# Where the gated layer takes the difference of candidate and old state: VectorE from PSUM, or GpSimd from SBUF

## The chip, the cores and the metric

The kernel runs on one core of one Trainium2 chip. The metric is the device time of one execution in microseconds (us), lower is better. Engines are named as in the profile: PE is TensorE (matmul), DVE is VectorE, ACT is ScalarE, POOL is GpSimd, SP is SyncE.

## The reference

Four layers work on `x` of 64 graphs x 256 nodes x 128 features, with one adjacency matrix `adj` of 256 x 256, all in fp32. Each layer normalizes over the features, applies a relu, runs a graph network and adds its result to `x`. Layer 0 is the gated one, with five steps; layers 1 and 2 multiply by `adj` and project; layer 3 scores every pair of nodes.

```python
# layer 0, five times; sigmoid and tanh gates
m  = einsum('nm,bmd->bnd', adj, h);  av = concatenate([m, m], -1)
u3 = h @ u3_w.T + u3_b
z  = sigmoid(av @ w3_w.T + w3_b + u3)
r  = sigmoid(av @ w4_w.T + w4_b + u3)
hv = tanh(av @ w5_w.T + w5_b + (r * h @ u5_w.T + u5_b))
h  = (1.0 - z) * h + z * hv            # = h + z * (hv - h)
...
# layer 3: s1, s2 are two projections of h, for each pair of nodes i, j
pre = s1[:, :, None, :] + s2[:, None, :, :] + b_lin
e   = einsum('bije,e->bij', leaky_relu(pre, 0.2), a) + adj
out = sigmoid(softmax(e, axis=2) @ h)
```

## The kernel before

Two graphs form a pair (`NB = 2`), so there are 32 pairs. For each pair a generator `front(p)` issues layers 0 to 2 and the projections of layer 3. It keeps the state of the gated layer as `hT`, features on partitions, 128 x 512 (two graphs of 256 nodes).

Then comes the bulk of the work, the pair scores of layer 3. For a pair of graphs there are 2 x 64 tiles `rl` of 128 x 2048 elements: the minimum or relu of a row of s1 against all of s2. A tile can be made by DVE in one instruction (L669), by ACT in eight (L682) or by POOL in eight (L689). PE multiplies a finished tile by the score vector in eight matmuls of 512 columns (L726). There are 13 tile buffers, of which DVE may hold 8, ACT 3 and POOL 2. When a block of rows is scored, a second generator `tail` does its softmax and writes the result.

One order of instructions for each engine is written out by a planner while the kernel is traced. It keeps a clock for each engine, books each operation with a cost (`ran(engine, us, ...)`; `ELEMENTS = 0.61` for an elementwise DVE operation on 512 columns, `TANH = 0.57`, 2.2 for a DVE tile, 1.8 for two of POOL's instructions), and always moves on the engine that is furthest behind. A `yield engine, t` in a generator means that its next operation goes to that engine and has its inputs at time t. Ready steps of a tail go first, then those of a front, the earlier pair first, and a tile only when no step is ready. So engines with little other work make more tiles. The fronts of later pairs are spread out between the tiles: a front has 109 steps, and step k is not given out before its due time, which spreads them over the scoring of 1.7 pairs, up to two steps ahead:

```python
    STEPS_OF_FRONT, SPREAD, AHEAD = 109, 1.7, 2
...
            due = STEPS_OF_FRONT * (scored[0] / (2 * SLOTS) - (key - 2)) / SPREAD
            if CHAINS[key][2] > due + AHEAD:
                return None
```

Fronts 0 and 1 start together before any tile exists. The others begin as the scoring goes on.

PSUM has eight banks of 128 x 512. Three of them (`spare`) rotate among all fronts and tails: `take()` gets one, `spare.append` gives it back with the time from which it is free. SBUF work tiles with `**SHORT` share 12 buffers.

In a step of the gated layer the bank `pr` holds first the reset gate's and then the update gate's sum, and `pv` the candidate's. ACT applies a tanh to each (L403 for the update gate, L406 for the candidate; the sigmoids are written as tanhs of half the argument). DVE takes the difference of candidate and old state (L411), multiplies it by the gate plus one (L415) and adds half of that to the old state, which gives the new `hT` (L419).

Of the kernel before, what the change touches and what calls it, by code (L numbers as in the profile page):

```python
# [9 lines left out]
AF = mybir.ActivationFunctionType  # L10
# [10 lines left out]
PE, DVE, ACT, POOL = ENGINES = (mybir.EngineType.PE, mybir.EngineType.DVE, mybir.EngineType.Activation, mybir.EngineType.Pool)  # L21
# [4 lines left out]
def kernel(  # L26
# [50 lines left out]
    nc = tc.nc  # L77
# [17 lines left out]
    clock = dict.fromkeys((PE, DVE, ACT, POOL), 0.0)  # L95
# [4 lines left out]
    def ran(engine, us, *after):  # L100
        start = max(clock[engine], 0.0, *after)
        if engine == ACT:
            behind[0] = max(0.0, behind[0] - (start - clock[ACT])) + 0.024 * us
        clock[engine] = start + us
        return clock[engine] + SEEN[engine] + (behind[0] if engine == ACT else 0.0)
# [6 lines left out]
    spare = [[b, 0.0] for b in banks[5:]]  # L112

    def take():

        spare.sort(key=lambda b: b[1])
        return spare.pop(0)

    def by_feature(b):
        return b.rearrange("p (b n) -> p b n", b=NB)  # L120

    def by_token(b):
        return b.rearrange("p (b c n) -> p b c n", b=NB, c=NC)
# [95 lines left out]
    bz, br, bh = gate_b[:, 0:1], gate_b[:, 1:2], gate_b[:, 2:3]  # L219
# [56 lines left out]
    def project(pp, w, t, start=True, stop=True):  # L276

        side_by_side(pp, w, flat(t), start, stop)

    def mix_nodes(pm, h, a):  # L280

        pm = by_feature(pm)
        for b in range(NB):
            for c in range(NC):
                side_by_side(pm[:, b, :], h[:, b, c, :], a[:, c, :], c == 0, c == NC - 1)
# [8 lines left out]
    def to_token(pt, ht):  # L294

        pt = by_token(pt)
        for b in range(NB):
            for c in range(NC):
                nc.tensor.transpose(pt[:, b, c, :], ht[:, b, c * P:(c + 1) * P], ident)  # L299
# [9 lines left out]
    def feat(name, **kw):  # L309
        return work.tile([P, NB, N], F32, name=name, **kw)  # L310

    def tok(name, **kw):
        return work.tile([P, NB, NC, D], F32, name=name, **kw)
# [8 lines left out]
    COPY, BIASED, TANH, ELEMENTS = 0.48, 0.58, 0.57, 0.61  # L322

    def norm(src, since, h):

        stats = work.tile([P, NB * NC, 6], F32, name="stats")
        mv = work.tile([P, NB * NC, 2], F32, name="mv")
        s, h = rows_of(src), rows_of(h)
        yield DVE, since
        for k in range(NB * NC):  # L330
            nc.vector.bn_stats(stats[:, k, :], s[:, k, :])  # L331
        for k in range(NB * NC):
            nc.vector.bn_aggr(mv[:, k, :], stats[:, k, :])  # L333
        nc.vector.tensor_scalar(mv[:, :, 0], mv[:, :, 0], -1.0, None, op0=OP.mult)  # L334
        t = ran(DVE, 1.12, since)
        yield POOL, t
        inverse_root(mv[:, :, 1], OP.add, LN_EPS)
        nc.gpsimd.tensor_mul(mv[:, :, 0], mv[:, :, 0], mv[:, :, 1])  # L338
        t = ran(POOL, 1.4, t)
        yield ACT, t  # L340
        for k in range(NB * NC):
            nc.scalar.activation(h[:, k, :], s[:, k, :], AF.Relu, bias=mv[:, k, 0:1], scale=mv[:, k, 1:2])  # L342
        return ran(ACT, 1.54, t)

    def copied(name, bank, t):

        c = feat(name, **(SHORT if name not in KEPT else KEPT[name]))
        nc.scalar.copy(c, by_feature(bank[0]))  # L348
        t = ran(ACT, COPY, t)
        spare.append([bank[0], t])  # L350
        return c, t
# [5 lines left out]
    def front(p):  # L357
# [8 lines left out]
        t = yield from norm(x0, 0.0, h)  # L366
# [4 lines left out]
        t = ran(PE, TURN, t, b[1])  # L371
        yield ACT, t
        hT, t_hT = copied("hT", b, t)
        for step in range(STEPS):
            yield PE, t_h, 1
            b = take()
            mix_nodes(b[0], h, adj_t)
            t = ran(PE, MIX, t_h, b[1])
            yield ACT, t
            mT, t_m = copied("mT", b, t)  # L380
            yield PE, t_m, 1
            pr = take()
            project(pr[0], u3t, hT, stop=False)
            project(pr[0], w4t, mT, start=False)
            t = ran(PE, 2 * PROJECT, t_m, t_hT, pr[1])
            yield ACT, t, 1
            r = take()
            nc.scalar.activation(r[0], pr[0], AF.Tanh, bias=br, scale=0.5)  # L388
            t = ran(ACT, TANH, t, r[1])
            yield DVE, t  # L390
            rh = feat("rh", **SHORT)
            nc.vector.scalar_tensor_tensor(rh, by_feature(r[0]), 1.0, hT, op0=OP.add, op1=OP.mult)  # L392
            t_rh = ran(DVE, ELEMENTS, t)
            spare.append([r[0], t_rh])
            yield PE, t_rh, 1
            project(pr[0], w34, mT, start=False)
            t_z = ran(PE, PROJECT, t)
            pv = take()
            project(pv[0], w5t, mT, stop=False)
            project(pv[0], u5t, rh, start=False)  # L400
            t = ran(PE, 2 * PROJECT, t_rh, pv[1])
            yield ACT, t_z
            nc.scalar.activation(pr[0], pr[0], AF.Tanh, bias=bz, scale=0.5)  # L403
            t_z = ran(ACT, TANH, t_z)
            yield ACT, t
            nc.scalar.activation(pv[0], pv[0], AF.Tanh, bias=bh, scale=1.0)  # L406
            t = ran(ACT, TANH, t)

            yield DVE, t
            d = feat("d", **SHORT)  # L410
            nc.vector.tensor_sub(d, by_feature(pv[0]), hT)  # L411
            t = ran(DVE, ELEMENTS, t)
            spare.append([pv[0], t])
            yield DVE, max(t_z, clock[DVE])
            nc.vector.scalar_tensor_tensor(by_feature(pr[0]), by_feature(pr[0]), 1.0, d, op0=OP.add, op1=OP.mult)  # L415
            ran(DVE, ELEMENTS, t_z)
            yield DVE, clock[DVE]
            hT_new = feat("hT", bufs=4)
            nc.vector.scalar_tensor_tensor(hT_new, by_feature(pr[0]), 0.5, hT, op0=OP.mult, op1=OP.add)  # L419
            hT = hT_new  # L420
            t_hT = ran(DVE, ELEMENTS)
            spare.append([pr[0], t_hT])
            yield PE, t_hT, 1
            b = take()
            to_token(b[0], hT)
            t = ran(PE, TURN, t_hT, b[1])
            if step < STEPS - 1:
                yield ACT, t
                h = tok("h", **SHORT)
                nc.scalar.copy(h, by_token(b[0]))  # L430
                t_h = ran(ACT, COPY, t)
                spare.append([b[0], t_h])
# [3 lines left out]
        t = ran(DVE, ELEMENTS, t)  # L436
# [8 lines left out]
        t = ran(PE, MIX, t_h, b[1])  # L445
# [5 lines left out]
        t = ran(PE, TURN, t_h, b[1])  # L451
        yield ACT, t
        hT, t = copied("hT", b, t)
# [3 lines left out]
        t = ran(PE, MIX, t_h, b[1])  # L457
        yield ACT, t
        c2T, t = copied("c2T", b, t)
# [3 lines left out]
        t = ran(PE, PRODUCTS, t, po[1])  # L463
# [7 lines left out]
        t = ran(DVE, ELEMENTS)  # L471
# [4 lines left out]
        t = yield from norm(x2, t, h)  # L476
# [3 lines left out]
        t = ran(PE, MIX, t, b[1])  # L480
        yield ACT, t
        yT, t = copied("yT", b, t)
# [3 lines left out]
        t = ran(PE, PRODUCT, t, po[1])  # L486
# [3 lines left out]
        t = ran(DVE, ELEMENTS, t)  # L490
# [3 lines left out]
        t = ran(ACT, COPY, t)  # L494
# [3 lines left out]
        t = ran(DVE, ELEMENTS, t)  # L498
        yield POOL, t
        inverse_root(rn, OP.max, NORM_EPS * NORM_EPS)  # L500
        t = ran(POOL, 1.25, t)
# [6 lines left out]
        t = ran(DVE, 1.04, t)  # L508
# [4 lines left out]
        t = yield from norm(x3, t, h3)  # L513
# [3 lines left out]
        t = ran(PE, TURN, t, b[1])  # L517
        yield ACT, t
        hT, t_hT = copied("hT3", b, t)
# [13 lines left out]
        t = ran(PE, 0.22, t_hT, b[1])  # L533
# [3 lines left out]
        t = ran(ACT, 0.2, t)  # L537
# [9 lines left out]
        t = ran(PE, PROJECT, t_hT, b[1])  # L547
# [5 lines left out]
        t = ran(PE, PROJECT, t_hT, b[1])  # L553
# [8 lines left out]
        t = ran(PE, PROJECT, t_hT, b[1])  # L562
# [180 lines left out]
    def begin_front():  # L743
        p = begun_fronts[0]
        load_x(p + 1)
        begin(p, front(p))
        begun_fronts[0] += 1
# [87 lines left out]
```

## Time and profile before

| | us |
|---|---|
| median of 3 runs (range) | 5335.91 (5334.29 to 5347.27) |
| profiled execution, its own time | 5333.93 |
| its span | 5332.2 |
| PE, DVE, ACT, POOL busy | 5222.4, 5206.3, 5123.7, 5140.8 |
| DVE tiles (L669), busy | 4469.3 in 2009 instructions |
| ACT tiles (L682), busy | 4410.4 + 149.3 in 11072 + 312 instructions |
| POOL tiles (L689), busy | 4765.8 in 5312 instructions |
| differences on DVE (L411), busy | 108.6 in 160 instructions |
| tanh of the candidate on ACT (L406), busy | 148.9 in 160 instructions |

A group's row names the line, the engine, the operation, the tiles written and read with their shapes and the count; then its busy time and the mean ns of one; then the idle time of the engine just before it and what ended it. Instructions of one engine overlap, so the mean length of one is more than what it takes of the engine's time.

### The profile page before, as it was taken

How to read it: one execution, taken by the hardware profiler on the slowest of the kernel's cores; microseconds unless marked ns; L12 is line 12 of the kernel's file. 1: busy time of each engine (PE TensorE's matmuls, PEld its weight loads, DVE VectorE, ACT ScalarE, POOL GpSimd, SP SyncE). 2: the span in 40 equal slices, each digit the busy share in tenths (PEclk: the TensorE clock that was granted, in tenths of full speed). 3: DMA queues.
4: the chain of work that ended last, by engine and by line, in shares of the span. 5: the costliest groups of instructions: out<-in, count | busy, mean ns of one | idle time of the engine just before them, and what ended most of it. 6: DMA issues, size and time to landing. Idle time of an engine off the chain costs nothing.

```text
span 5332.2 us, 139121 instructions
## 1 busy us (share of the span) xinstructions
PE 5222.4 (98%) x56085; PEld 1864.0 (35%) x56085; DVE 5206.3 (98%) x4316; ACT 5123.7 (96%) x13529; POOL 5140.8 (96%) x5958
## 2 busy tenths in 40 slices
PE   7999999999999999999999999999999999999998
PEld 2333333333333333333333333333333333333332
DVE  3999999999999999999999999999999999999998
ACT  3999999999999999999999999999999999999998
POOL 0999999999999999999999999999999999999999
PEclk8999999999999999999999999999999999999999
DMA  0000000000000000000000000000000000000000
GB/s 17 10 5 8 8 5 8 8 5 8 8 5 8 5 8 8 5 8 7 6 8 7 6 8 5 8 8 5 8 8 5 8 7 6 8 5 6 6 5 4
DMA packets 60344, 37.49 MB, mean 7 GB/s; under 512 B 4528, under 2 KB 59696, under 8 KB 59696
## 3 DMA queue, kind: packets, MB, share of 16 engines
q1 hardware_dynamic: 56592, 27.54, 2.3%
q8 instruction: 438, 7.18, 0.6%
q14 instruction: 210, 1.72, 0.1%
q10 hardware_dynamic: 3104, 1.05, 0.1%
HBM read 18.09 MB, written 10.49 MB: 5 GB/s over the span
## 4 chain that ended last, share of the span: by engine, by line
DVE 52%; PE 27%; POOL 12%; issue 6%; ACT 2%; DMA 0%; DVEq 0%; POOLq 0%; SPq 0%; ACTq 0%
DVE rl L669 43%; PE bank L726 17%; POOL rl L689 11%; PE bank L271 9%; ACT rl L682 2%; DVE bank L415 1%; DVE hT L419 1%; DVE d L411 1%; DVE stats L331 1%; DVE rh L392 1%; PE bank L299 1%; DVE mv L334 1%; DVE nmx L583 1%; DVE mv L333 0%; POOL mv L266 0%
## 5 line engine op out<-in xcount | busy, mean ns | idle before, releaser
L689 POOL TENSOR_SCALAR rl<-s2n,s1b 128x256 f32<-128x256 f32 x5312 | 4765.8, 928 | 9.2 <-ACT s1b L556 8.9
L669 DVE TENSOR_TENSOR rl<-s1a,bank 128x2048 f32<-128x2048 f32 x2009 | 4469.3, 2276 | 11.2 <-ACT s1a L565 11.2
L682 ACT ACTIVATE rl<-bank,s1b 128x256 f32<-128x256 f32 x11072 | 4410.4, 913 | 1.0
L726 PE MATMUL bank<-rl,win_n 128*32 128x512 f32 x21384 | 2647.7, 593 | 38.6 <-DVE rl L669 34.3
L726 PE MATMUL bank<-rl,win 128*32 128x512 f32 x11384 | 1503.3, 593 | 0.0
L726 PEld LDWEIGHTS bank<-rl,win_n 128*32 128x32 f32 x21384 | 680.9, 110 | 1509.6 <-issue 1203.9
L726 PEld LDWEIGHTS bank<-rl,win 128*32 128x32 f32 x11384 | 367.8, 110 | 749.2 <-issue 627.1
L271 PE MATMUL bank<-adj_t,h 128*32 128x256 f32 x5120 | 308.7, 381 | 3.9 <-ACT h L430 3.8
L271 PEld LDWEIGHTS bank<-adj_t,h 128*32 128x32 f32 x5120 | 166.2, 110 | 173.7 <-issue 54.8
L342 ACT ACTIVATE h<-x,mv 128x128 f32<-128x128 f32 x384 | 173.7, 653 | 35.4 <-POOL mv L338 35.0
L348 ACT COPY mT<-bank 128x512 f32<-128x512 f32 x160 | 147.6, 922 | 37.1 <-PE bank L271 28.0
L271 PE MATMUL bank<-hT,u3t 128*32 128x512 f32 x1280 | 167.6, 593 | 0.0
L271 PE MATMUL bank<-mT,w4t 128*32 128x512 f32 x1280 | 167.6, 592 | 0.0
L271 PE MATMUL bank<-mT,w 128*32 128x512 f32 x1280 | 166.8, 593 | 0.5 <-ACT bank L388 0.5
L271 PE MATMUL bank<-mT,w5t 128*32 128x512 f32 x1280 | 166.8, 593 | 0.3 <-DVE rh L392 0.2
L388 ACT ACTIVATE bank<-bank,gate_b 128x512 f32<-128x512 f32 x160 | 152.4, 953 | 14.8 <-PE bank L271 14.4
L271 PE MATMUL bank<-rh,u5t 128*32 128x512 f32 x1280 | 166.6, 592 | 0.0
L403 ACT ACTIVATE bank<-bank,gate_b 128x512 f32<-128x512 f32 x160 | 147.8, 924 | 13.3 <-PE bank L271 13.2
L406 ACT ACTIVATE bank<-bank,gate_b 128x512 f32<-128x512 f32 x160 | 148.9, 930 | 11.2 <-PE bank L271 11.0
L430 ACT COPY h<-bank 128x512 f32<-128x512 f32 x128 | 132.2, 1032 | 23.3 <-PE bank L299 23.2
L682 ACT ACTIVATE rl<-s2c,s1a 128x256 f32<-128x256 f32 x312 | 149.3, 902 | 0.0
L411 DVE TENSOR_TENSOR d<-bank,hT 128x512 f32<-128x512 f32 x160 | 108.6, 678 | 37.6 <-ACT bank L406 37.6
(116 smaller groups left out, 3319.9 us busy)
## 6 DMA issues: line engine op xcount, KB each, us to landing
xin<-in_x_dram SPq DMA_DIRECT2D x64, 128.0 KB, 2.3
lin<-row SPq DMA_DIRECT2D x32, 256.0 KB, 7.6
out_dram<-o SPq DMA_DIRECT2D x64, 128.0 KB, 1.8
row<-quarter SPq DMA_DIRECT2D x32, 64.0 KB, 1.5
w_raw<-in_L_gnn_w_w_dram ACTq DMA_DIRECT2D x3, 128.0 KB, 4.1
th_raw<-in_L_gnn_Theta_dram ACTq DMA_DIRECT2D x1, 320.0 KB, 3.4
adj_n<-in_adj_dram SPq DMA_DIRECT2D x1, 256.0 KB, 4.5
w_raw<-in_L_gnn_u_w_dram ACTq DMA_DIRECT2D x2, 64.0 KB, 3.3
```

Of the source, the lines that this page charges most:

```text
L271: nc.tensor.matmul(o[g:g + 32], w[:, g:g + 32], t, start=start, stop=stop, skip_group_check=True)
L342: nc.scalar.activation(h[:, k, :], s[:, k, :], AF.Relu, bias=mv[:, k, 0:1], scale=mv[:, k, 1:2])
L348: nc.scalar.copy(c, by_feature(bank[0]))
L388: nc.scalar.activation(r[0], pr[0], AF.Tanh, bias=br, scale=0.5)
L403: nc.scalar.activation(pr[0], pr[0], AF.Tanh, bias=bz, scale=0.5)
L406: nc.scalar.activation(pv[0], pv[0], AF.Tanh, bias=bh, scale=1.0)
L411: nc.vector.tensor_sub(d, by_feature(pv[0]), hT)
L430: nc.scalar.copy(h, by_token(b[0]))
L669: nc.vector.tensor_tensor(t, rows.to_broadcast(whole), ops["s2a"].unsqueeze(1).to_broadcast(whole), op=OP.min)
L682: nc.scalar.activation(t[:, g, b, :], (s2p if k else ops["s2c"])[:, b, :], AF.Relu, bias=ops["s1"][k][:, b, i:i + 1], scale=-1.0)
L689: nc.gpsimd.tensor_scalar(t[:, part, b, :], ops["s2n"][:, b, :], ops["s1"][1][:, b, i:i + 1], None, op0=OP.min)
L726: nc.tensor.matmul(pe[g * 32:(g + 1) * 32, :], w[:, k, 31 - r:63 - r], flat(t[:, g]), start=first, stop=(left[block] == 0), skip_group_che ...
```

## The change

For all pairs but the first, ACT writes the candidate's tanh to the SBUF tile `d` instead of back into the PSUM bank `pv`, and gives the bank back at that point. GpSimd, which the kernel has read and write SBUF alone, subtracts the old state from `d` in place. DVE's product follows, planned at the later of that and the update gate's tanh. The planner books the subtraction with 1.3 us on POOL. Pair 0 stays as it was.

```diff
             nc.scalar.activation(pr[0], pr[0], AF.Tanh, bias=bz, scale=0.5)
             t_z = ran(ACT, TANH, t_z)
             yield ACT, t
-            nc.scalar.activation(pv[0], pv[0], AF.Tanh, bias=bh, scale=1.0)
-            t = ran(ACT, TANH, t)
-
-            yield DVE, t
+
             d = feat("d", **SHORT)
-            nc.vector.tensor_sub(d, by_feature(pv[0]), hT)
-            t = ran(DVE, ELEMENTS, t)
-            spare.append([pv[0], t])
-            yield DVE, max(t_z, clock[DVE])
+            if p < 1:
+                nc.scalar.activation(pv[0], pv[0], AF.Tanh, bias=bh, scale=1.0)
+                t = ran(ACT, TANH, t)
+                yield DVE, t
+                nc.vector.tensor_sub(d, by_feature(pv[0]), hT)
+                t = ran(DVE, ELEMENTS, t)
+                spare.append([pv[0], t])
+            else:
+                nc.scalar.activation(d, by_feature(pv[0]), AF.Tanh, bias=bh, scale=1.0)
+                t = ran(ACT, TANH, t)
+                spare.append([pv[0], t])
+                yield POOL, t
+                nc.gpsimd.tensor_sub(d, d, hT)
+                t = ran(POOL, 1.3, t)
+            yield DVE, max(t, t_z)
             nc.vector.scalar_tensor_tensor(by_feature(pr[0]), by_feature(pr[0]), 1.0, d, op0=OP.add, op1=OP.mult)
-            ran(DVE, ELEMENTS, t_z)
+            ran(DVE, ELEMENTS, t, t_z)
             yield DVE, clock[DVE]
             hT_new = feat("hT", bufs=4)
             nc.vector.scalar_tensor_tensor(hT_new, by_feature(pr[0]), 0.5, hT, op0=OP.mult, op1=OP.add)
```

The number of steps of a front stays 109.

## The prediction

> **What bounds the kernel now.** I read the page first: its span, the busy row and the costliest groups.
>
> ```profile
> span 5332.2 us, 139121 instructions
> PE 5222.4 (98%) x56085; PEld 1864.0 (35%) x56085; DVE 5206.3 (98%) x4316; ACT 5123.7 (96%) x13529; POOL 5140.8 (96%) x5958
> L689 POOL TENSOR_SCALAR rl<-s2n,s1b 128x256 f32<-128x256 f32 x5312 | 4765.8, 928 | 9.2 <-ACT s1b L556 8.9
> L669 DVE TENSOR_TENSOR rl<-s1a,bank 128x2048 f32<-128x2048 f32 x2009 | 4469.3, 2276 | 11.2 <-ACT s1a L565 11.2
> L682 ACT ACTIVATE rl<-bank,s1b 128x256 f32<-128x256 f32 x11072 | 4410.4, 913 | 1.0
> L411 DVE TENSOR_TENSOR d<-bank,hT 128x512 f32<-128x512 f32 x160 | 108.6, 678 | 37.6 <-ACT bank L406 37.6
> ```
>
> All four engines look full. Three of them make the same thing, pair tiles for the attention scores, and the planner gives the next tile to whichever is free. A tile is one instruction on DVE and eight on ACT or POOL: 2009 + 1423 + 664 = 4096 tiles. Work taken off one engine is therefore refilled with tiles, and the question is the exchange rate. Next, the sums by stretch:
>
> ```profile
> core 0: us, PE busy (x) PEld busy (x) DVE busy (x) ACT busy (x) POOL busy (x), PEclk, DMA share, GB/s
> 1066.00:2132.00 1066.00, 1059.36 (x11424) 376.01 (x11426) 1062.65 (x870) 1047.34 (x2772) 1052.04 (x1218) 1.00 0.03 7
> 2132.00:3198.00 1066.00, 1057.77 (x11498) 378.60 (x11494) 1061.81 (x878) 1039.71 (x2751) 1055.11 (x1223) 1.00 0.03 7
> ```
>
> Between the start (no tiles before 113 us) and the last 270 us, DVE is 99.6% busy, POOL 98.8%, ACT about 98%, at full clock. Matmul busy time is no peak, so I counted PE's work at the pace of its unbroken runs in the timeline: 0.857 us per tile's eight 512-column matmuls, 1.73 per 32 of 256 columns, 0.90 per 32 of 128, 0.58 per four transposes. With the counts of the groups: 4305 + 443 + 180 + 186 = 5114 us. Taking out the first 133 us and the ragged last 270, PE has about 100 us (2%) to spare in the long stretch. DVE and POOL set the pace, PE is close behind.
>
> Durations overlap, so prices must come from start to next start. The timeline of DVE (start, length, ...):
>
> ```profile
> 2518.71 6.67 DVE L669 TENSOR_TENSOR rl<-s1a,bank 128x2048 f32<-128x2048 f32 x3
> 2525.30 0.16 DVE L609 RECIPROCAL rs<-sums 128x2 f32<-128x2 f32 x1
> 2525.38 0.67 DVE L411 TENSOR_TENSOR d<-bank,hT 128x512 f32<-128x512 f32 x1
> 2525.96 2.28 DVE L669 TENSOR_TENSOR rl<-s1a,bank 128x2048 f32<-128x2048 f32 x1
> ...
> 5001.14 0.68 DVE L411 TENSOR_TENSOR d<-bank,hT 128x512 f32<-128x512 f32 x1
> 5001.86 0.70 DVE L415 SCALAR_TENSOR_TENSOR bank<-bank,d 128x512 f32<-128x512 f32 x1
> ```
>
> A DVE tile is (2525.30 − 2518.71)/3 = 2.197 us. The difference takes 0.60 before other work (0.58 here; 0.60 is usual), and 0.72 when the product that reads it comes straight after. POOL and ACT in the same way:
>
> ```profile
> 2516.78 1.30 POOL L579 TENSOR_TENSOR sc<-sc,lin 128x512 f32<-128x512 f32 x1
> 2518.03 12.57 POOL L689 TENSOR_SCALAR rl<-s2n,s1b 128x256 f32<-128x256 f32 x14
> ...
> 2522.02 1.13 ACT L406 ACTIVATE bank<-bank,gate_b 128x512 f32<-128x512 f32 x1
> 2522.59 1.08 ACT L597 ACTIVATE wT<-bank 128x512 f32<-128x512 f32 x1
> ...
> 2531.16 1.37 ACT L556 ACTIVATE s1b<-bank,blin 128x512 f32<-128x512 f32 x1
> 2531.73 3.71 ACT L682 ACTIVATE rl<-bank,s1b 128x256 f32<-128x256 f32 x8
> 2534.58 1.44 ACT L565 ACTIVATE s1a<-bank,blin 128x512 f32<-128x512 f32 x1
> ```
>
> A POOL tile is 8 × 12.57/14 = 7.18 us, its two-input 128x512 add 1.25, an ACT tile 2534.58 − 2531.73 = 2.85.
>
> **The change part by part.** It touches pairs 1 to 31 at five steps each, 155 times. In the trace ten differences run before the first tile: five of pair 0 (unchanged) and five of pair 1, where DVE and POOL both stand idle much of the time. That leaves 150 in the tile stretch.
>
> *Removed from DVE.* In the DVE timeline 67 of the 150 are followed directly by their product (mean 0.71), 83 by other work (0.60): 47.8 + 49.7 = 97.5 us, or 97.5/2.197 = 44.4 tiles.
>
> *Added to POOL.* Its subtraction of two SBUF inputs isn't in the trace, but the add of the same shape and operands is (L579, 1.26 to 1.35 long, while DVE was saturated). I take its 1.25 us; the bounds are 1.15 and 1.40. 150 × 1.25 = 188 us = 26.1 tiles. Here a rule speaks against the change: the Trainium skill, "GPSIMD Engine Reference", section "Engine selection", wants elementwise work on VectorE, since two-input operations are about 2 times slower on GpSimd. The rows agree on the ratio (1300/678 = 1.92). By the rule alone the move adds 188 − 97.5 = 90 us of engine time, +30 us over three engines. But that treats all engine time as equal: on tiles POOL is 7.18/2.197 = 3.3 times slower than DVE, so POOL is better at the subtraction than at what it otherwise does. I go by the rows: +44.4 − 26.1 = +18.3 tiles.
>
> *ACT's tanh into SBUF.* The nearest rows by destination are the biased activations s1a and s1b: mean 1195 and 1109 ns against 930 for L406. The Trainium skill, "ScalarE: Activation LUTs", section "Step-by-step: what each stage is for", says that ScalarE reaches PSUM faster than SBUF. Priced by these means, 0.18 to 0.27 × 150 = 27 to 40 us of ACT, 9 to 14 tiles, most of the gain. But start to next start it is 0.57 for L406 and 0.57 for s1b: the difference is latency, covered by the next activation. I take 0, with +0.1 (15 us, 5 tiles) as the bad end and −0.05 as the good one; the latency is met again below.
>
> *Rate.* Making tiles at 1/2.197 + 1/7.18 + 1/2.85 = 0.945 per us, 18.3 tiles are 19.4 us.
>
> *New waits.* DVE's product now waits for POOL, with tiles and the next rows of gates queued behind it; POOL's subtraction waits for ACT, with its quarter tiles behind it; PE waits for both. Nearest row: DVE's maximum waiting for POOL's add in the long stretch, second line below. That is 3.2 us for some 62, 0.05 each, where the planner books 1.05 us against 1.25 measured; the subtraction is booked at 1.3. I take 0.03 × 150 = 4.5 us of DVE, 2 tiles, 2 us; the bounds are 0 and 0.18 (ACT waiting for POOL's norm, first line, 22.2 us for some 125).
>
> ```profile
> ACT h L342 <- POOL mv L338: 22.2, 28, 2.7
> ...
> DVE nmx L583 <- POOL sc L579: 3.2, 10, 0.8
> ```
>
> *Latency and banks.* The chain of a step gets about 2 to 3 us longer (1.3 on POOL, a partial POOL tile ahead of it, and the product must queue for DVE). I cost this at nothing: 109 steps of a front are spread over 1.7 pairs of scoring, about 2.5 us a step, and the tiles between product and new state in the timeline show chains being held back, not rushed. Were that cover gone, 5 × 2.5 us per pair would delay READY, and DVE would stop before L669; it does so once, at the start. The candidate's bank comes free after the tanh instead of after the difference, the update gate's is held about as much longer: even. No DMA moves, so SP's queue is untouched. Startup: pair 0 unchanged, 0.
>
> Sum: −19.4 + 2 = −17.4 us against the profiled execution's own 5333.9 (span 5332.2), so 5316.5. The median of runs is 2 us above it: 5319.
>
> **The rivals.**
> *More than the sum.* The plan books 0.61 for a difference that took 0.71 in 67 cases, so DVE runs behind its plan and PE waits for it: PE's loads waited 99.3 us for DVE tiles in the long stretch (209 times, of which about 0.3 each is mere pace) and 61.9 for the new state. If the change saves 15 us of these as well, 5304. Against: POOL takes on the same role.
> *PE and ACT take it up.* PE has 2% to spare, yet in the chain of waits it runs unbroken for tens of us. ACT idles about 100 us in the long stretch, much of it before copies out of banks that PE has not filled. If faster DVE production only adds to that, or the tanh costs ACT 0.1 more, half or less of the gain is left: 5326 to 5336.
> *POOL comes late (slower).* One mechanism: POOL almost never waits, so each delay on it lasts, and DVE now meets it 150 times. The exchange breaks even when DVE idles 18.3 × 2.197/150 = 0.27 us per product. If half a POOL instruction is lost each time (0.9/2 = 0.45), DVE loses 67 us, 31 tiles, and the kernel is +13 us: 5349. For it: 12 of 64 maxima already waited for POOL. Against: 0.05 us each.
> The edit does what it says for 31 of 32 pairs, so that it has no effect at all I give no share.
>
> **How the numbers follow.** Differences under 0.3% (16 us) can hardly be told from none here: the three runs lie within 13 us. The sum of the parts: 0.55, its own range 5309 to 5327; the line of 0.3% is at 5319.9, so 0.33 of it is faster and 0.22 the same. More than the sum: 0.17, faster. PE and ACT: 0.17, same. POOL late: 0.11, slower. Together 0.50, 0.39, 0.11. The range 5302 to 5338 leaves out POOL late and the far end of the gain.
>
> **What would show it.** Right: L411's subtraction as 155 POOL rows near 1300 ns and 5 on DVE; DVE tiles up by about 35 to 45 to some 2050, POOL's fall from 664 to about 640, ACT's nearly unchanged; DVE still over 99% busy; DVE's product waiting for POOL under 10 us; the tanh's next activation still 0.57 later. Wrong: the product waiting over 40 us for POOL; ACT's tiles falling by 15 or more; the POOL row over 1.5 us, or POOL tiles slower than 0.90 per instruction, which would mean that DVE slows it; more PE waits before banks.

## The result and the profile after

The changed kernel takes 5323.38 us (median of 14 runs, 5321.42 to 5333.19) against 5335.67 us for the kernel before (14 runs), a ratio of 0.9978 with a 95% interval of 0.9971 to 0.9985. That is 12.3 us or 0.23%: clear of noise, but on the near side of the 0.3% line.

Executions come in two paces of ACT and POOL, 0.1 to 0.3% apart as the last section shows, and the kernel's time differs by 7 to 13 us between them, so executions of the same pace are set against each other below. The profile of the changed kernel shown here (from the run after2) is of the faster pace, like that of before: span 5322.4 us, own time 5324.2 us.

The page's busy row, its costliest groups, and then ACT's smaller group of tiles, before (L682) and after (L690):

```profile
PE 5211.6 (98%) x56085; PEld 1855.6 (35%) x56085; DVE 5189.9 (98%) x4198; ACT 5092.5 (96%) x13465; POOL 5126.3 (96%) x5881
...
L697 POOL TENSOR_SCALAR rl<-s2n,s1b 128x256 f32<-128x256 f32 x5080 | 4559.9, 923 | 16.0 <-ACT s1b L564 9.5
L677 DVE TENSOR_TENSOR rl<-s1a,bank 128x2048 f32<-128x2048 f32 x2046 | 4545.1, 2275 | 11.9 <-ACT s1a L573 11.9
L690 ACT ACTIVATE rl<-bank,s1b 128x256 f32<-128x256 f32 x11304 | 4511.0, 893 | 2.0 <-PE bank L734 0.8
...
L682 ACT ACTIVATE rl<-s2c,s1a 128x256 f32<-128x256 f32 x312 | 149.3, 902 | 0.0
L690 ACT ACTIVATE rl<-s2c,s1a 128x256 f32<-128x256 f32 x16 | 7.6, 838 | 0.0
```

Counts are the first thing to read. DVE makes 2046 tiles instead of 2009, POOL 5080/8 = 635 instead of 664, and ACT the rest: 4096 − 2046 − 635 = 1415 instead of 1423. So DVE gains 37, POOL loses 29, and ACT loses 8.

The tiles are not quite one pool. They come in two halves of 2048, one for each half of the score's features (0 and 1), and the planner chooses the half for an engine:

```python
        return 0 if e == DVE or e == ACT and following[0] <= following[1] - LAG else 1
```

DVE makes tiles of half 0 only and POOL of half 1 only. ACT helps with half 0 when that is at least two tiles behind (`LAG = 2`). For those tiles it reads SBUF (`s2c`), for its others a PSUM bank. ACT made 312/8 = 39 tiles of half 0 before and makes 16/8 = 2 now, so DVE does its half nearly alone. By the medians from start to start in unbroken runs of tiles, an instruction of the SBUF form takes 399 ns and one of the PSUM form 356, so the 37 tiles fewer spare ACT 37 × 8 × 43 ns = 12.7 us.

Next the subtraction and what stands around it, from the groups of instructions by shape:

```profile
L420 POOL TENSOR_TENSOR d<-d,hT 128x512 f32<-128x512 f32 x155 | 199.9, 1290 | 67.5 <-ACT d L416 67.5
L416 ACT ACTIVATE d<-bank,gate_b 128x512 f32<-128x512 f32 x155 | 162.3, 1047 | 9.1 <-PE bank L271 9.0
...
L423 DVE SCALAR_TENSOR_TENSOR bank<-bank,d 128x512 f32<-128x512 f32 x160 | 110.4, 690 | 17.7 <-POOL d L420 17.3
```

155 subtractions of 1290 ns sit on POOL, as priced by the row of the score add. POOL's 67.5 us of idle time before them lie at the start, where it has nothing else to do. In the long stretch the waits are tiny (who waited, for whom: us, times, longest):

```profile
DVE bank L423 <- POOL d L420: 1.3, 5, 0.4
...
POOL d L420 <- ACT d L416: 1.1, 2, 0.6
```

The steps in the timeline, ACT's tanh and POOL's subtraction of one chain:

```profile
2549.22 1.03 ACT L416 ACTIVATE d<-bank,gate_b 128x512 f32<-128x512 f32 x1
2549.78 9.21 ACT L690 ACTIVATE rl<-bank,s1b 128x256 f32<-128x256 f32 x24
...
2552.18 1.28 POOL L420 TENSOR_TENSOR d<-d,hT 128x512 f32<-128x512 f32 x1
2553.44 7.19 POOL L697 TENSOR_SCALAR rl<-s2n,s1b 128x256 f32<-128x256 f32 x8
```

The tanh is longer than before, yet ACT's next activation starts 0.56 us after it (the median of 150 is 0.57, as before). POOL gives 1.26 us to the subtraction. Finally the long stretch by engine. First the kernel before, then the changed one:

```profile
133.00:5065.00 4932.00, 4892.88 (x52939) 1746.09 (x52935) 4911.33 (x4042) 4827.85 (x12763) 4876.95 (x5647) 1.00 0.03 7
```

```profile
133.00:5065.00 4932.00, 4896.07 (x53080) 1750.52 (x53084) 4912.61 (x3945) 4802.73 (x12714) 4869.02 (x5580) 1.00 0.03 7
```

The five busy times are PE, PE's weight loads, DVE, ACT and POOL. DVE's idle time is the same (4932 − 4911.3 = 20.7 us and 19.4). ACT's grew from 104.2 to 129.3 us (129.2 in a profile of the slower pace). This is where the experiments began.

### The profile page after: what moved, and what is told of

Its sections match the earlier page's. It is cut to its first block, busy times and chain, and to the rows that moved or that the text cites. A ratio compares the mean times of both kernels' runs of the same rounds, so it can differ in the third digit from the quotient of the medians.

```text
span 5331.4 us, 138379 instructions
## 1 busy us (share of the span) xinstructions
PE 5217.8 (98%) x56085; PEld 1858.3 (35%) x56085; DVE 5195.0 (97%) x4198; ACT 5101.5 (96%) x13465; POOL 5137.7 (96%) x5881
## 3 DMA queue, kind: packets, MB, share of 16 engines
q8 instruction: 438, 7.18, 0.6%
## 4 chain that ended last, share of the span: by engine, by line
DVE 41%; PE 37%; POOL 12%; issue 5%; ACT 4%; DMA 0%; POOLq 0%; DVEq 0%; SPq 0%; ACTq 0%
DVE rl L677 34%; PE bank L734 24%; PE bank L271 12%; POOL rl L697 11%; ACT rl L690 3%; DVE stats L331 1%; PE bank L299 1%; DVE hT L427 1%; DVE bank L423 1%; DVE rh L392 1%; DVE mv L334 1%; PE bank L292 0%; POOL d L420 0%; DVE nmx L591 0%; DVE sc L583 0%
## 5 line engine op out<-in xcount | busy, mean ns | idle before, releaser
L697 POOL TENSOR_SCALAR rl<-s2n,s1b 128x256 f32<-128x256 f32 x5080 | 4574.9, 942 | 14.9 <-ACT s1b L564 9.3
L677 DVE TENSOR_TENSOR rl<-s1a,bank 128x2048 f32<-128x2048 f32 x2046 | 4544.9, 2275 | 11.6 <-ACT s1a L573 11.6
L690 ACT ACTIVATE rl<-bank,s1b 128x256 f32<-128x256 f32 x11304 | 4520.1, 903 | 2.1 <-PE bank L734 0.9
L420 POOL TENSOR_TENSOR d<-d,hT 128x512 f32<-128x512 f32 x155 | 203.4, 1313 | 68.5 <-ACT d L416 68.5
L403 ACT ACTIVATE bank<-bank,gate_b 128x512 f32<-128x512 f32 x160 | 160.4, 1002 | 28.7 <-PE bank L271 28.5
L348 ACT COPY mT<-bank 128x512 f32<-128x512 f32 x160 | 141.1, 882 | 43.2 <-PE bank L271 21.6
L416 ACT ACTIVATE d<-bank,gate_b 128x512 f32<-128x512 f32 x155 | 164.5, 1061 | 9.3 <-PE bank L271 9.2
L388 ACT ACTIVATE bank<-bank,gate_b 128x512 f32<-128x512 f32 x160 | 151.4, 946 | 14.9 <-PE bank L271 10.6
L438 ACT COPY h<-bank 128x512 f32<-128x512 f32 x128 | 124.5, 973 | 21.6 <-PE bank L299 18.2
L266 POOL TENSOR_TENSOR mv<-mv,minus_half 128x4 f32<-128x4 f32 x128 | 133.2, 1041 | 10.7
```

Source lines behind the costliest of these rows:

```text
L266: nc.gpsimd.tensor_tensor(t, t, minus_half, op=OP.pow)
L416: nc.scalar.activation(d, by_feature(pv[0]), AF.Tanh, bias=bh, scale=1.0)
L420: nc.gpsimd.tensor_sub(d, d, hT)
L677: nc.vector.tensor_tensor(t, rows.to_broadcast(whole), ops["s2a"].unsqueeze(1).to_broadcast(whole), op=OP.min)
L690: nc.scalar.activation(t[:, g, b, :], (s2p if k else ops["s2c"])[:, b, :], AF.Relu, bias=ops["s1"][k][:, b, i:i + 1], scale=-1.0)
L697: nc.gpsimd.tensor_scalar(t[:, part, b, :], ops["s2n"][:, b, :], ops["s1"][1][:, b, i:i + 1], None, op0=OP.min)
```

## The experiments

Theory 1 (exchange): DVE, ACT and POOL set the pace, and whatever time one of them is spared becomes tiles at the rates of the prediction. Theory 2: PE is so near to full, or booked as so near to full, that the planner holds ACT back when DVE makes more tiles, and part of the gain ends as idle time of ACT. A tile waits in its buffer for PE, and ACT may hold three.

**The same kernel again.** No edit, for a profile at the pace of before.

> The changed kernel once more, for a second profile (the first profiled execution, 5333.2 us, lay 10 us above the median of the runs). Theory 1 (exchange: DVE, ACT and POOL all set the pace and freed time becomes tiles): about 5323 us again, ACT idle in the stretch 133 to 5065 us close to the 104 us of before. Theory 2 (PE, as the planner books it, is already full, so the planner holds ACT back): the same time, but ACT idle 20 to 40 us more than before.

Measured: 5324.2 us at the faster pace against 5335.9 for before on the same chip (11.6 us less), 5333.4 against 5348.9 at the slower one (15.5 us less). ACT idle in the stretch is 129.3 us in this execution, 25 us more than before, as theory 2 has it; the slower profile had shown as much, so this repeats a reading and tests nothing new.

**The subtraction left out.** DVE is relieved, POOL pays nothing.

```diff
-                yield POOL, t
-                nc.gpsimd.tensor_sub(d, d, hT)
-                t = ran(POOL, 1.3, t)
...
-    STEPS_OF_FRONT, SPREAD, AHEAD = 109, 1.7, 2
+    STEPS_OF_FRONT, SPREAD, AHEAD = 104, 1.7, 2
```

> The changed kernel with the subtraction left out for pairs 1 to 31: the product reads the tanh itself (front of 104 steps, so that the spread stays). DVE is relieved as in the change and POOL pays nothing. Theory 1: 44 tiles / 0.945 per us = 47 us under before, 5289 us. Theory 2: freed time ends as idle time of ACT; 10 to 25 us under before (5311 to 5326), ACT idle up by 80 us or more.

Measured: 5316.4 us at the faster pace (one execution, 19.5 us under before), 5323.7 at the slower (25.2 under). Theory 1 fails: less than half of the 47 us came. Its profile says where the rest went:

```profile
133.00:5065.00 4932.00, 4901.69 (x53198) 1755.98 (x53202) 4912.49 (x3949) 4751.89 (x12551) 4858.37 (x5627) 1.00 0.03 7
```

ACT idles 4932 − 4751.9 = 180.1 us, 76 more than before (theory 2 had 80 or more). At 2.85 us a tile that is 26.7 tiles, or 26.7/0.945 = 28 us of the kernel. The gap between 47 and 19.5 is 27.5.

**The other half alone.** POOL pays, DVE is not relieved.

```diff
+            if p >= 1:
+                yield POOL, t
+                e = feat("e", **SHORT)
+                nc.gpsimd.tensor_sub(e, d, hT)
+                ran(POOL, 1.3, t)
             yield DVE, max(t_z, clock[DVE])
...
-    STEPS_OF_FRONT, SPREAD, AHEAD = 109, 1.7, 2
+    STEPS_OF_FRONT, SPREAD, AHEAD = 114, 1.7, 2
```

> The kernel before, and beside its difference on DVE a second one on POOL for pairs 1 to 31 into a tile that nothing reads (front of 114 steps). POOL pays as in the change and DVE is not relieved. Theory 1: 26.1 tiles / 0.945 = 28 us over before, 5363 us. Theory 2: ACT was being held back and takes the tiles over; 10 to 22 us over before, ACT idle below 104 us.

Measured: 5371.0 us, 22.1 over before at the same (slower) pace, at the upper end of what theory 2 had and under the 28 of theory 1. ACT makes 1438 tiles instead of 1423, but its idle time falls only from 104 to 97 us. At this pace −25.2 and +22.1 add to −3, while the change itself brings −15.5. With fixed exchange rates the two halves would add up to the change; they don't.

**PE booked at the trace's pace.** Only the planner's numbers change, on the changed kernel, on the kernel before, and on the changed kernel a second time.

```diff
-    PROJECT, MIX, TURN, PRODUCT, PRODUCTS = 0.86, 1.74, 0.69, 0.88, 2.64
+    PROJECT, MIX, TURN, PRODUCT, PRODUCTS = 0.855, 1.715, 0.59, 0.875, 2.62
```

> The changed kernel with PE's operations booked in the planner at the pace that the trace shows (0.855, 1.715, 0.59, 0.875, 2.62 instead of 0.86, 1.74, 0.69, 0.88, 2.64); the work is the same. Theory 1: no change, within 5 us of 5323. Theory 2: the planner sees room on PE and lets ACT make more tiles: 10 to 25 us faster than the change (5298 to 5313), ACT idle falls by 30 us or more.

Measured: 5323.7 us at the slower pace, 9.7 us under the changed kernel there. ACT idle is 97.5 us instead of 129.3. The order alone is worth 10 us, as theory 2 says.

> The kernel before with PE's operations booked in the planner at 0.855, 1.715, 0.59, 0.875, 2.62. Compared with the changed kernel so booked, and with the kernel before at the same pace of ACT and POOL. Theory 2 (the tight booking of PE is what eats part of the change's gain): before gains less from the new booking than the changed kernel's 10 us, 0 to 5 us, and the change is then worth 17 to 22 us. Rival: the booking helps both alike, before gains 8 to 12 us, and the change stays worth 10 to 15 us.

> The changed kernel with that booking once more, to stand beside pe_before on the same chip. Theory 2: 17 to 22 us under pe_before. Rival: 10 to 15 us under it.

Measured, both at the slower pace: the kernel before goes from 5346.6 to 5339.3 us (7.3 less; ACT idle 86.7 us in its profile, which is of the faster pace), the changed one to 5323.6. So the change is worth 15.7 us with the new booking and 15.5 with the old one. Here my expectation failed: the loose booking costs both kernels about alike and is not what ate the change's gain. If theory 2 holds, it must be through PE's real load.

**PE made lighter.** One product of the gated layer is left out in all pairs (137 us of PE work in all): in the kernel before, in the changed kernel, and in the one without the subtraction.

```diff
-            project(pr[0], w34, mT, start=False)
-            t_z = ran(PE, PROJECT, t)
+            t_z = t_rh
```

> The kernel before with one PE product of the gated layer left out in all pairs (the update gate's w34 times mT, eight 512-column matmuls a step, 160 x 0.858 = 137 us of PE). It is the base for light_after and light_nodiff. Theory 2 in its wider form (PE is so close to full that the queue of finished tiles in front of it holds ACT back): 10 to 20 us faster than before, ACT idle in the stretch down from 104 us to 90 or less. Theory 1: no more than 3 us faster, since PE isn't what sets the pace.

> The changed kernel with the same PE product left out. Theory 2: with room on PE the change keeps what the exchange rates give, 15 to 20 us under light_before, and ACT's idle time no longer grows with it. Theory 1: the same 12 to 15 us as without the lighter PE.

> no_diff (the subtraction left out for pairs 1 to 31, tanh into SBUF) with the same PE product left out. This tells the theories apart best: with PE as it was, leaving the subtraction out was worth 20 to 25 us instead of the 47 us of the exchange. Theory 2: 40 to 50 us under light_before, ACT idle not above light_before's by more than 15 us. If something other than PE holds ACT back: again 20 to 28 us, with ACT idle up by 60 us or more.

All ran at the faster pace, with before at 5335.7 us:

| with the lighter PE | us | to light_before | the same edit with full PE, faster pace | ratio to before (95%) |
|---|---|---|---|---|
| light_before | 5324.5 | | | 0.9980 (0.9972 to 0.9987) |
| light_after | 5302.9 | −21.6 | −12.3 | 0.9938 (0.9925 to 0.9950) |
| light_nodiff | 5276.5 | −48.1 | −19.5 | 0.9889 (0.9876 to 0.9903) |

The long stretch of light_before, then of light_after, then of light_nodiff:

```profile
133.00:5065.00 4932.00, 4809.39 (x51820) 1727.27 (x51816) 4916.24 (x4050) 4846.79 (x12827) 4875.94 (x5647) 1.00 0.03 7
```

```profile
133.00:5065.00 4932.00, 4830.18 (x52060) 1742.98 (x52056) 4913.70 (x3942) 4854.23 (x12869) 4876.32 (x5589) 1.00 0.03 7
```

```profile
133.00:5065.00 4932.00, 4838.33 (x52224) 1738.41 (x52220) 4913.28 (x3956) 4849.91 (x12852) 4882.95 (x5656) 1.00 0.03 7
```

ACT idles 85.2, 77.8 and 82.1 us: taking DVE's subtraction away no longer lets ACT run dry. Without it the kernel gains 48.1 us, where the exchange rates say 47. The lighter PE by itself brings the kernel before 11.1 us, and its ACT idle from 104.2 to 85.2. So the exchange rates are right, and with 2.6% less work on PE they are paid out.

How PE's load reaches ACT is not shown. That it is the limit of three held tiles is read from the planner's rules; it was not changed by itself. The rule for the halves is another candidate: ACT may take DVE's work only when half 1 is two tiles ahead, and it made 2 such tiles in no_diff, as in the changed kernel, but 24 in light_nodiff. A larger `LAG` is tried below, a smaller one was not. In the trace of no_diff ACT's waits stand before activations of fronts and tails: norms wait 51.3 us for POOL (22.2 before), and tiles only 3.0 for PE. The edit that lightens PE also takes one wait away directly, that of the update gate's tanh for the product left out. It cost ACT 21.7 us in the changed kernel and 8.5 before, which is half of the change's growth, but only 15.3 of 180 us in no_diff. And PE's load is not all: with PE's full work the order alone brought the changed kernel's ACT idle to 97.5 us (pe_after) and 84.0 (spread, below).

**The subtraction on DVE, from SBUF.** This keeps the tanh's new destination and takes POOL out.

```diff
-                yield POOL, t
-                nc.gpsimd.tensor_sub(d, d, hT)
-                t = ran(POOL, 1.3, t)
+                yield DVE, t
+                nc.vector.tensor_sub(d, d, hT)
+                t = ran(DVE, ELEMENTS, t)
```

> The changed kernel with the subtraction put back on DVE, now from the tile that ACT's tanh has written to SBUF (two SBUF inputs on DVE). It keeps the tanh's new destination and takes the move to POOL away. If the tanh into SBUF costs ACT nothing: within 5 us of before, and the tanh's step to the next activation 0.57. If it costs 0.03 us each (5 us of ACT): 0 to 3 us slower than before. Where DVE's two inputs from SBUF and POOL's reads hinder each other, the difference is longer than 0.68 or POOL's instructions longer than 0.93, and the kernel 5 to 40 us slower than before.

Measured: 5385.8 us, 39.2 over before at the same (slower) pace, a ratio of 1.0073 (1.0060 to 1.0086). Its two operations (duration in ns: minimum/median/maximum):

```profile
L420 DVE TENSOR_TENSOR d<-d,hT x155: 662/693/1158, 42.4 to 5079.1; 128x512 f32<-128x512 f32 x155
```

```profile
L697 POOL TENSOR_SCALAR rl<-s2n,s1b x5320: 908/937/1481, 139.7 to 5369.1; 128x256 f32<-128x256 f32 x198
```

In the kernel before, where the same difference read one input from PSUM, its longest instance was 692 ns and POOL's longest 960 (1015 in the changed kernel at the slower pace). All 102 POOL instructions over 1100 ns lie beside such a subtraction. Two inputs from SBUF on DVE stretch instructions of both engines by up to half a microsecond. The Trainium skill, "SBUF — State Buffer", section "Who interferes with whom", states this conflict between a DVE instruction with two SBUF inputs and a GpSimd instruction that reads SBUF; this run shows it. The lengthening adds up to some 14 us on DVE (767 ns mean against 678, 155 times) and, from about 100 POOL steps over 950 ns, 37 us on POOL. By the exchange rates that is (14/2.197 + 37/7.18)/0.945 = 12 us. The other 27 us are about what the added waiting is worth: in the long stretch ACT idles 146.0 us instead of 104.2 and DVE 43.0 instead of 20.7, by the same rates (41.8/2.85 + 22.3/2.197)/0.945 = 26 us. (The profile of before is of the faster pace; in the changed kernel the two paces differ by 0.1 us of ACT's idle time and 3.5 of DVE's.) What starts that waiting stays open. So the subtraction from SBUF could not stay on DVE without this cost. The change itself shows no such conflict (POOL's longest tile instruction in its profile is 961 ns): DVE's product takes the gate from PSUM. On the open question of the tanh, the median step to the next activation is 0.57 us here too.

**Two tries for a faster order.**

```diff
# lag4: pe_after2 and
-    LAG = 2
+    LAG = 4
# spread: lag4 and
-    STEPS_OF_FRONT, SPREAD, AHEAD = 109, 1.7, 2
+    STEPS_OF_FRONT, SPREAD, AHEAD = 109, 1.9, 1
```

> pe_after2 with one more setting of the planner: ACT takes tiles of DVE's half of the pairs only when that half is 4 tiles ahead instead of 2 behind the other (LAG 4 for 2). A try for a faster version: 0 to 4 us under pe_after2 if ACT's held-back time comes from taking tiles that PE gets to late; no change if not.

> A try for a version faster than both: the changed kernel with PE booked as in pe_after, fronts spread over 1.9 pairs of scoring with one step ahead (1.7 and 2 before) and LAG 4. If bursts of front work on PE are what fills the queue of tiles, spreading them gives ACT back 15 to 25 us: 4 to 10 us under pe_after2. If not: within 3 us of it.

Measured: lag4 5321.6 us at the slower pace, 2 us under pe_after2 and 25.0 under before. spread 5312.7 us at the faster pace: 23.0 us under before, ratio 0.9958 (0.9944 to 0.9971), and 10.7 under the change. pe_after2 ran only at the slower pace, where it is 23.0 under before. So both tries are faster than both kernels, but most of what they gain over the changed kernel is the new booking of PE (9.7 us in pe_after). How much is the spreading's own can't be told without a run of pe_after2 at the faster pace; ACT idle is down to 84.0 us in its profile.

## Why the prediction was right or wrong

*The likeliest course was right in kind, and its size too large.* The sum was −17.4 us (5319); measured is −12.3 (5323.4), inside the range and inside the range of this course itself. The chances leaned to more than 0.3%, and it came to 0.23%.

*The prices held.* Subtraction on POOL 1.26 us in the timeline (taken: 1.25), tanh into SBUF with the next activation 0.56 later (taken: no cost). Tiles: DVE +37 (35 to 45 expected), POOL at 635 (about 640).

*New waits: over-priced.* The product waited 1.3 us for POOL in the long stretch, not 4.5. POOL late, the slower rival, has no sign in the profile.

*Latency and startup at nothing: nearly right.* DVE's first tile came at 140.5 us instead of 138.6, but 1.0 us of that was there at 19 us, before any changed instruction.

*Rate: the step that was mis-sized.* I counted 18.3 tiles at 0.945 per us as if ACT, too, would go on at its pace. I had the rival to this in the text (PE and ACT take it up) and the 2% that PE has to spare, and weighed them too low. ACT idled 25.1 us more in the long stretch, at the prediction's rates 25.1/2.85/0.945 = 9.3 us of the kernel. Against this stands a gain that I had not counted, since I took the tiles for one pool: ACT makes 37 tiles fewer of its slower form, 12.7 us of ACT or 4.7 us of the kernel. The two leave 4.6 us lost, near the missing 5.1. That they half cancel is luck, and part of why the number came so near. The over-priced waits go the other way by about 1.5 us, and some 2 us in all stay unexplained.

With PE lighter by 137 us the same change is worth 21.6 us, about 4 more than my sum. There ACT idled 7.4 us less with the change (2.7 us by the same rates) and made 12 tiles of the slower form instead of 44 (4.1 us), which is enough for the difference. With PE as it is, relieving DVE alone paid 19.5 of 47.

*The rule against the move* that the prediction cites (elementwise work belongs on VectorE) would have given +30 us by itself. The chip gave −12.3 and, with room on PE, −21.6: the comparison with what each engine does otherwise was the right one.

*More than the sum* didn't come. PE's loads did wait less in the long stretch (77.6 us for DVE's tiles instead of 99.3, and 56.1 for the new state instead of 61.9), but the time shows nothing of it.

## What to carry to other kernels

When engines share a pool of work, price a move by what each engine would otherwise produce: an operation may go to the engine that is slower at it if that engine is slower still at the shared work. Then ask whether the consumer of the pool can take the extra output: here PE had about 2% to spare on average, and part of the gain ended as idle time of one producer. Look also at whether each producer may make every item: here DVE could take over only what others made of its own half. Removing work from the consumer for one experiment tells whether it is the limit.

## What the runs showed of the hardware

The same program took 5324 and 5333 us. Three groups of the execution at the slower pace:

```profile
L697 POOL TENSOR_SCALAR rl<-s2n,s1b 128x256 f32<-128x256 f32 x5080 | 4574.9, 942 | 14.9 <-ACT s1b L564 9.3
L677 DVE TENSOR_TENSOR rl<-s1a,bank 128x2048 f32<-128x2048 f32 x2046 | 4544.9, 2275 | 11.6 <-ACT s1a L573 11.6
L690 ACT ACTIVATE rl<-bank,s1b 128x256 f32<-128x256 f32 x11304 | 4520.1, 903 | 2.1 <-PE bank L734 0.9
```

Against the rows shown for the faster one (4559.9, 4545.1 and 4511.0 us), POOL and ACT are longer and DVE is not. By the medians from start to start in unbroken runs of tiles, ACT's step is 356 ns in the faster executions and 357 in the slower ones, POOL's 895 and 896 to 897, while DVE's 2198 and PE's 858 per tile are the same in both. So 0.1 to 0.3% on two engines goes with 0.2% of this kernel's time, which is as much as the change itself. What sets the pace is not shown.

A second point is ACT's source: the same 128x256 relu took 399 ns from start to start where it read SBUF and 356 where it read PSUM (260 and 10005 steps in the kernel before).
